# Offsets, features and sampled keys by chunks of channels, in small steps inside the main loop, with the depthwise taps on VectorE

## The chip, the cores and the metric

The kernel runs on one core of one Trainium2 chip. The metric is the device time of one execution in microseconds; each figure is a median of several executions. All executions used here are in the fast state. "TensorE" is PE in the profile, "VectorE" is DVE, "ScalarE" is ACT, "GpSimd" is POOL. SBUF and PSUM are the on-chip memories that hold the kernel's tiles: its matmuls write PSUM tiles, and an "evacuation" is the ScalarE instruction that takes a finished PSUM tile to SBUF, with its ReLU (1.11 to 1.20 us each in the kernel before). The "granted clock" of a view is the share of TensorE's full clock that the profile shows.

## The reference, cut to what matters

The input has 2 images, 512 channels, 32 by 32 pixels. A depthwise 6x6 convolution with stride 4 over the queries gives offsets. At the offset positions the normalised input is sampled (64 keys per group). A bias network of two hidden layers of 128 runs on every pair of a pixel and a key, and that is nearly all the work.

```python
xn  = bn(x); q = grouped_1x1(xn, qw)
off = gelu(depthwise_6x6_stride4(q) + b)        # the 36 taps
off = tanh(off_pw @ off) * 4
kv  = grid_sample(xn, grid + off); k, v = ...   # the sampling
pos = grid_q - grid_kv
bias = sign(pos) * log1p(abs(pos))              # the features
bias = relu(bias @ w1 + b1); bias = relu(bias @ w2 + b2); bias = bias @ w3 + b3
attn = softmax(q k^T * scale + bias); x = x + out(attn v); x = x + mlp(bn(x))
# then one full attention layer over the 1024 pixels
```

## The kernel before

Everything up to the features is done for all channels at once, ahead of the main loop. The depthwise convolution is 36 matmuls with diagonal weights:

```python
for b in range(B):
    for k in range(NCH):          # 8 chunks of 128 channels: normalise, q, transposes
        ...
pc = pp.tile([P, 512], F32, tag="ps", name="pc")
for t in range(KS * KS):          # 36 taps on TensorE (72 in the profile)
    dg = ph2.tile([P, P], F32, name="dg", bufs=4)
    nc.vector.tensor_scalar(dg, ident, col("dww", t), None, ALU.mult)
    ky, kx = divmod(t, KS)
    nc.tensor.matmul(pc.rearrange(...), dg, qpad[:, :, ky : ky + 29 : 4, kx : kx + 29 : 4],
                     start=(t == 0), stop=(t == KS * KS - 1))
... # gelu, offsets, weights, sampling, keys, values, features; all chunks
```

The main loop has 256 steps. This is its order in both kernels:

```python
for s in range(NS):
    if s > 0: st_sum(s - 1, 2)                    # VectorE, 2nd sum of the step before
    if s % 4 == 0: st_tables(s // 4 + 1)          # DMA + two ScalarE ops: ta, tb (2 buffers)
    st_layer1(s + 2)                              # VectorE: h1 of 4096 elements (3 buffers)
    st_layer2(s)                                  # TensorE: 32 matmuls; ScalarE evacuates 4 PSUM tiles
    st_sum(s, 0)                                  # VectorE, 1st sum
    ...                                           # every 2nd step: layer 3; per group: softmax
```

The evacuations write `rx` (3 buffers), `ua` (5) and `ub` (4); three PSUM tiles of 128x1024 f32 serve layer 2 and, in the changed kernel, the background work too. Each matmul of the program appears as two MATMUL instructions in these profiles (16384 for layer 2, which is 256 steps of 32). The order in which an engine runs its instructions needn't be the order of the text: in the kernel before, VectorE ran a sign test of line 163 at 4.95 us and the first normalisation of line 118 at 7.48. Where it is said below that the build puts an instruction first or early, such an order is meant; by what rule it comes about, no run here shows.

## Time and profile before

| | before |
|---|---|
| time, median of 3 executions | 2977.14 us |
| head, up to the first layer-2 matmul | 180.66 us |
| loop, first layer-2 matmul to the end of the last | 1908.2 us |
| rest (projections, MLP, second layer) | 887.9 us |

The three parts below the first line are read from the profiled execution, which spans 2976.7 us. The profile's group lines give busy time in us and the mean of one instruction in ns, then the engine's idle time just before these instructions and what ended most of it. The lines themselves are shown in the prediction. The reading in one sentence: TensorE has no idle time in the loop (1908.20 us busy of 1908.20), and VectorE has half a microsecond to spare in a step (0.48 us, as the prediction works it out).

### The profile page before, as it was taken

What the parts mean: (1) busy time and instruction counts of PE and PEld (TensorE: products, weight loads), DVE (VectorE), ACT (ScalarE), POOL (GpSimd) and SP (SyncE); (2) the same over time, 40 slices, a digit from 0 to 9 for tenths busy, and PEclk for the clock granted to TensorE, in tenths of its full rate; (3) what the DMA queues carried; (4) which work ended last, traced back from release to release, by engine and by line L of the source; (5) the groups of instructions that cost most, each with busy time, mean ns of one, the idle gap of its engine ahead of it and who ended that gap; (6) DMA issues with size and microseconds to landing.
All of it is one profiled execution on the core that took longest, in us unless ns stands there. A gap on an engine that the chain in (4) does not pass through costs nothing.

```text
span 2976.7 us, 45771 instructions
## 1 busy us (share of the span) xinstructions
PE 2916.3 (98%) x20316; PEld 1059.9 (36%) x20316; DVE 1971.8 (66%) x1200; ACT 1439.9 (48%) x1381; POOL 221.3 (7%) x264
## 2 busy tenths in 40 slices
PE   8679999999999999999999999999999999999999
PEld 3323333333333333333333333335444444454444
DVE  3389999999999999999999999998200100013031
ACT  1346766666666766666667676666201011010010
POOL 0001111111111111111111111111000000000000
PEclk9889999999999999999999999999999999999999
DMA  2024444444444444444444444444200100000000
GB/s 89 0 61 93 86 96 83 93 86 93 86 93 86 93 86 93 86 93 86 93 86 93 85 92 88 89 106 111 113 0 0 57 0 0 0 0 1 28 1 29
DMA packets 59893, 197.48 MB, mean 66 GB/s; under 512 B 10288, under 2 KB 10544, under 8 KB 58544
## 3 DMA queue, kind: packets, MB, share of 16 engines
q0 software_dynamic: 36576, 133.19, 23.6%
q1 hardware_dynamic: 22544, 60.04, 6.9%
q8 instruction: 160, 2.62, 0.4%
q10 hardware_dynamic: 576, 1.34, 0.1%
q14 instruction: 37, 0.30, 0.0%
HBM read 56.91 MB, written 4.46 MB: 21 GB/s over the span
## 4 chain that ended last, share of the span: by engine, by line
PE 97%; DVE 1%; ACT 1%; DMA 0%; SPq 0%; issue 0%; ACTq 0%; DVEq 0%
PE ps L358 59%; PE psm L514 7%; PE psh L506 7%; PE sim L394 4%; PE pss L586 4%; PE psa L636 4%; PE pc L149 2%; PE psp L575 2%; PE pso L486 2%; PE psv L625 2%; PE psg L551 1%; PE pkv L242 1%; PE psq L123 1%; PE sim L384 1%; PE psx L605 0%; PE psu L560 0%
## 5 line engine op out<-in xcount | busy, mean ns | idle before, releaser
L358 PE MATMUL ps<-h,cw 128*32 128x512 f32 x16384 | 1792.9, 593 | 17.8 <-DVE h L341 17.8
L341 DVE CUSTOM_DVE_ANT_1 h<-ta,tb 128x4096 f32<-128x4096 f32 x256 | 1132.6, 4425 | 119.0 <-PE ps L358 102.3
L358 PEld LDWEIGHTS ps<-h,cw 128*32 128x32 f32 x16384 | 554.0, 110 | 1225.4 <-issue 1186.4
L364 ACT ACTIVATE rx<-ps,sc 128x1024 f32<-128x1024 f32 x512 | 570.2, 1114 | 326.5 <-PE ps L358 325.8
L366 ACT ACTIVATE ua<-ps,sc 128x1024 f32<-128x1024 f32 x256 | 308.3, 1204 | 152.5 <-PE ps L358 152.5
L366 ACT ACTIVATE ub<-ps,sc 128x1024 f32<-128x1024 f32 x256 | 307.9, 1203 | 115.3 <-PE ps L358 115.3
L374 POOL DMA_DIRECT2D ua<-ub x254 | 218.6, 861 | 1856.2 <-DVE ub L372 1840.2
L372 DVE SCALAR_TENSOR_TENSOR ua<-rx,sc,ua 128x1024 f32<-128x1024 f32 x256 | 327.6, 1280 | 14.4 <-ACT ua L366 14.1
L372 DVE SCALAR_TENSOR_TENSOR ub<-rx,sc,ub 128x1024 f32<-128x1024 f32 x256 | 327.3, 1279 | 5.6 <-ACT ub L366 5.6
L518 DVE SCALAR_TENSOR_TENSOR xs<-psm,vs,xs 128x512 f32<-128x512 f32 x16 | 12.0, 752 | 425.7 <-PE psm L514 425.7
L506 PE MATMUL psh<-xn,w_s 128*128 128x512 f32 x512 | 220.4, 592 | 0.0
L514 PE MATMUL psm<-hm,w_s 128*128 128x512 f32 x512 | 220.4, 592 | 0.0
L510 ACT ACTIVATE hm<-psh,vs 128x512 f32<-128x512 f32 x64 | 44.0, 687 | 364.0 <-PE psh L506 364.0
L506 PEld LDWEIGHTS psh<-xn,w_s 128*128 128x128 f32 x512 | 97.3, 190 | 122.4 <-issue 122.4
L514 PEld LDWEIGHTS psm<-hm,w_s 128*128 128x128 f32 x512 | 97.3, 190 | 122.4 <-issue 122.4
L394 PE MATMUL sim<-ua,w3s 128*32 128x512 f32 x1024 | 136.7, 593 | 0.0
L586 PE MATMUL pss<-xs,qs 128*128 128x512 f32 x256 | 112.2, 592 | 0.0
L636 PE MATMUL psa<-aT,vt 128*128 128x512 f32 x256 | 110.2, 592 | 0.0
L327 ACT ACTIVATE ta<-fb,vs 128x512 f32<-128x512 f32 x64 | 89.7, 1401 | 20.9 <-DMA fb<-fdr 16.1
L592 DVE TENSOR_REDUCE mx<-pss 128x1 f32<-128x1024 f32 x16 | 19.6, 1225 | 117.8 <-PE pss L586 117.8
L579 ACT ACTIVATE qs<-psp,ub 128x512 f32<-128x512 f32 x16 | 11.0, 687 | 137.8 <-PE psp L575 137.8
L641 DVE SCALAR_TENSOR_TENSOR res<-psa,ub,xs 128x512 f32<-128x512 f32 x16 | 12.0, 751 | 97.3 <-PE psa L636 97.3
(134 smaller groups left out, 1051.0 us busy)
## 6 DMA issues: line engine op xcount, KB each, us to landing
ua<-ub POOLq DMA_DIRECT2D x254, 512.0 KB, 4.7
fb<-fdr SPq DMA_DIRECT2D x64, 512.0 KB, 5.3
w_s<-in_w SPq DMA_DIRECT2D x8, 1024.0 KB, 12.1
x<-in_x SPq DMA_DIRECT2D x8, 512.0 KB, 8.0
xs<-in_x SPq DMA_DIRECT2D x16, 256.0 KB, 6.8
wl_s<-in_wl SPq DMA_DIRECT2D x4, 1024.0 KB, 7.9
out<-res SPq DMA_DIRECT2D x16, 256.0 KB, 2.0
vp<-in_outw SPq DMA_DIRECT2D x1, 1024.0 KB, 9.3
```

The costliest lines, as they stand in the source:

```text
L327: nc.scalar.activation(ta.rearrange("p j x -> p x j"), fb[:, 0], AF.Identity, bias=col("cb1"), scale=col("w1x"))
L341: nc.vector._custom_dve(TENSOR_ADD_SAT, out=h1.rearrange("p y t x -> p (y t x)"), in0=ta[:, j : j + 4, :].rearrange("p t x -> p (t x)").un ...
L358: nc.tensor.matmul(ps[32 * q : 32 * q + 32, h, :], cw2[:, 32 * z : 32 * z + 32], h1[:, 16 * h : 16 * h + 16, q, :], start=True, stop=True,)
L364: nc.scalar.activation(o, ps, AF.Relu, bias=sc[:, 4 + z : 5 + z])
L366: nc.scalar.activation(o, ps, AF.Relu, bias=sc[:, 4 + z : 5 + z], scale=sc[:, z : z + 1])
L372: nc.vector.scalar_tensor_tensor(r[1], r[0], sc[:, z : z + 1], r[1], ALU.mult, ALU.add)
L374: nc.gpsimd.dma_start(out=sums[s][1], in_=sums[s][3], accum_op=ALU.add)
L394: nc.tensor.matmul(sims[gi][q : q + 32, :], w3s[:, 28 - 4 * i : 60 - 4 * i], sums[s + e][z][:, h, :], start=False, stop=(i == NSL // 2 - 1 ...
L506: nc.tensor.matmul(ps, w1_s[:, k, i * P : (i + 1) * P], xn2[:, k, :], start=(k == 0), stop=(k == NCH - 1),)
L514: nc.tensor.matmul(ps, w2_s[:, i, o * P : (o + 1) * P], hm[:, i, :], start=(i == 0), stop=(i == NF - 1),)
L586: nc.tensor.matmul(ps[:, h, :], qs[:, k, t * P : (t + 1) * P], xs[:, k, b, h * 512 : (h + 1) * 512], start=(k == 0), stop=(k == NCH - 1),)
L636: nc.tensor.matmul(ps, vt[:, m, o * P : (o + 1) * P], aT[:, m, n], start=(m == 0), stop=(m == 7),)
```

## The change

The intent is to start the loop as soon as the first 128 channels have their features, and to do the other seven chunks' work beside the loop, in the slack of the other engines. The channels are split into five chains (one, one, two, two, two chunks). A generator does a little of the work in each step of the loop. The taps become multiply-add operations of VectorE on the SBUF copy of q.

```diff
+CHAINS = [[(0, 0)], [(0, 1)], [(0, 2), (0, 3)], [(1, 0), (1, 1)], [(1, 2), (1, 3)]]
+TAPS = 3
-        for t in range(KS * KS):
-            nc.vector.tensor_scalar(dg, ident, col("dww", t), None, ALU.mult)
-            nc.tensor.matmul(pc.rearrange(...), dg, qpad[...], ...)
+        def chain(ci):                      # load, normalise, q, taps, gelu, offsets, features
+            ...
+            for m, t in enumerate(taps):
+                for src, dst in ops:        # qa in steps of 4 pixels; two ops at the y edges
+                    if m == 0:
+                        nc.vector.tensor_scalar(dst, src, col("dww", t), None, ALU.mult)
+                    else:
+                        nc.vector.scalar_tensor_tensor(dst, src, col("dww", t), dst, ALU.mult, ALU.add)
+                if ci > 0 and m % (2 * TAPS // K) == 2 * TAPS // K - 1:
+                    yield                   # 6 taps a step for one chunk, 3 for two
+            ...
+        def sample(ci): ...                 # weights, transposes, sampling, keys, values
+        def later():
+            yield from sample(0)
+            for ci in range(1, len(CHAINS)):
+                yield from chain(ci)
+                yield from sample(ci)
+        for _ in chain(0): pass             # only the first chunk ahead of the loop
 ...
+        bg = later()
         for s in range(NS):
             ...
             st_sum(s, 0)
+            next(bg, None)
```

Small preparations (weight signs, scales) move from VectorE to GpSimd, and the products of q and k close a group's accumulation instead of opening it.

## The prediction

> **What bounds the kernel now.** I read the page first, then five windows, then single stretches of the order in time.
>
> The engine rows and the costliest groups of the page:
> ```profile
> PE 2916.3 (98%) x20316; PEld 1059.9 (36%) x20316; DVE 1971.8 (66%) x1200; ACT 1439.9 (48%) x1381; POOL 221.3 (7%) x264
> L358 PE MATMUL ps<-h,cw 128*32 128x512 f32 x16384 | 1792.9, 593 | 17.8 <-DVE h L341 17.8
> L341 DVE CUSTOM_DVE_ANT_1 h<-ta,tb 128x4096 f32<-128x4096 f32 x256 | 1132.6, 4425 | 119.0 <-PE ps L358 102.3
> ```
> TensorE is busy throughout; its largest group waited 17.8 us in all, VectorE waited 102.3 us for TensorE. I then cut the span at the taps, the end of the taps, the first layer-2 matmul and the last layer-3 matmul (start:end, length, then busy us and instructions of each engine, granted clock, DMA share, GB/s):
> ```profile
> 0.00:34.30 34.30, 23.67 (x96) 14.29 (x96) 22.40 (x96) 10.80 (x18) 2.71 (x10) 1.00 0.49 192
> 34.30:100.40 66.10, 66.10 (x75) 15.31 (x74) 10.20 (x34) 1.24 (x2) 0.00 (x0) 1.00 0.00 0
> 100.40:180.60 80.20, 35.87 (x308) 25.24 (x306) 43.39 (x41) 34.87 (x43) 0.00 (x0) 0.74 0.07 17
> 180.60:2092.50 1911.90, 1911.19 (x17652) 603.07 (x17652) 1781.53 (x843) 1309.06 (x1195) 218.61 (x254) 1.00 0.45 90
> 2092.50:2976.70 884.20, 879.47 (x2191) 402.01 (x2188) 114.29 (x189) 83.97 (x126) 0.00 (x0) 0.99 0.05 19
> ```
> So there are 180.6 us of head: 34 of loading and q, 66 of the depthwise taps as 72 TensorE matmuls, 80 of offsets, sampling and features with TensorE less than half busy. Then the loop: 256 steps in 1911.9 us, 7.47 us each, with no TensorE idle. Last comes the rest, also TensorE. Whatever TensorE work moves into the loop is therefore paid in full; whatever moves to the other engines costs only what exceeds their slack.
>
> That slack, in VectorE's order over two steps:
> ```profile
> 430.52 4.43 DVE L341 CUSTOM_DVE_ANT_1 h<-ta,tb 128x4096 f32<-128x4096 f32 x1
> 434.86 1.28 DVE L372 SCALAR_TENSOR_TENSOR ub<-rx,sc,ub 128x1024 f32<-128x1024 f32 x1
> 436.06 1.28 DVE L372 SCALAR_TENSOR_TENSOR ua<-rx,sc,ua 128x1024 f32<-128x1024 f32 x1
> 438.24 4.43 DVE L341 CUSTOM_DVE_ANT_1 h<-ta,tb 128x4096 f32<-128x4096 f32 x1 [0.91 <-PE ps L358]
> ```
> VectorE works 6.9 us of a step and waits 0.91 us in every second one, for TensorE to free an h1 buffer. Between 280 and 2000 us its groups' idle sums to 110 us over 231 steps: 0.48 us a step, softmax included. ScalarE's busy time in the loop, 1309 of 1912 us, leaves 2.3 us a step.
>
> The end of the head, which stays in the changed kernel:
> ```profile
> 164.83 2.85 SPq L300 DMA_DIRECT2D fdr<-late  x4
> ...
> 174.41 1.25 ACT L327 ACTIVATE ta<-fb,vs 128x512 f32<-128x512 f32 x1 [12.64 <-DMA fb<-fdr]
> ...
> 180.66 1.08 PE L358 MATMUL ps<-h,cw 128*32 128x512 f32 x4 [17.78 <-DVE h L341]
> ```
> From the write of the features to the first layer-2 matmul: 15.8 us of write, broadcast read, tables and first h1.
>
> [...] the three-operand operation takes 0.751 us for 512 elements (L641) and 1.280 for 1024 (L372), 1.033 ns an element and 0.222 us fixed. [...] each load here takes 1283 ns. Each chain adds a Gelu and an Ln set and softmax comes back to Exp. [...] the first four q matmuls took 3.75 us, later fours 1.88.
>
> **The change part by part.**
>
> *New head.* Only chunk (0,0) goes through it.
> - x, 512 KB: similar transfers in the loop land in 4.7 to 5.3 us; with 0.7 of issue and company, ready at 6.0 us. Normalisation on ScalarE 1.1: 7.2. Four cold q matmuls 3.8: 11.0. One copy of 1024 elements 1.1: 12.1.
> - 36 taps, each needing the one before. A dependent pair starts 0.03 after the first ends (L214 starts at 105.96 for 1.23, L218 on its result at 107.22). So 0.222 + 64 x 1.033 ns + 0.03 = 0.32; 36 of them, 11.4 us: 23.5.
> - Gelu 0.3, six small projections on a cool TensorE 1.2, two tanh 0.7, offsets 1.3: 27.0. Features on 128 columns instead of 1024: pos, Abs, u 0.8; then Ln with its load (1.6) beside the reciprocal chain (reciprocal 6.54 us per 1024, so about 1.0 here; 1.9 in all); two closing operations 0.7: 30.4.
> - The 15.8 us above, 0.7 less for a smaller write: first layer-2 matmul at **45.5 us**, instead of 180.66.
>
> GpSimd now takes 67 sign/swap operations and the BN scale. [...]
>
> *The fixed rest.* From 180.66 to 2976.7: **2796.0 us**, the same work.
>
> *TensorE work moved into the loop,* per chunk: q four matmuls at 0.44 (L273: 7.03/16) 1.76; eight transposes 1.04; pkv 32 x 0.068 (16.51/242) 2.18; kv keys 2 x 0.12 = 0.25; values 0.88: 6.1 us, 48.9 for eight. Less what runs before the loop starts, when TensorE is free (q and sampling of chunk 0, q of chunk 1): 7.9. Plus four sets of projections 2.4, and the first group's q.k products, which used to precede 180.66, 0.9. Sum **44 us**. The 66 us of tap matmuls vanish and are inside the head already.
>
> *VectorE in the loop.* Taps: chain 1 11.4. A two-chunk chain has 24 merged taps of 128 elements at 0.385 and 12 edge taps of two operations, about 0.5 a pair: 15.2 us, three times. Weights 7 x 1.23 = 8.6; offsets and features about 6.6 for each large chain and 4 for the small one. Sum about 11 + 46 + 9 + 24 = 90 us, spread by the count of yields over steps 0 to 105. Slack there: 106 x 0.48 = 51, plus the 44 that TensorE gains: 95. It just fits in total, but not at every moment: twelve tap steps bring 15.2/12 = 1.27 us against 0.48, a lag of 9.5 us; the feature steps bring about 3 more. The buffers absorb a part: h1 is made at least a step early (h1 of step s+2 starts when step s does, needs 4.4 of 14.9 us), but rx has three buffers, so a sum delayed by some 7 us stops ScalarE, then PSUM. So about 4 us lost in each of three large chains, 2 in the small one: 14. ScalarE pieces of 1.1 us and eight or more table loads ahead of evacuations, 3 more. **17 us**.
>
> *End.* The new xs lies over h1 and tables, not over qpad, so x is loaded at the loop's end instead of earlier. Such a load takes 6.8 us; the first product needs it about 5 us after the loop, and there are three PSUM buffers: **1 us**.
>
> Sum: 45.5 + 2796.0 + 44 + 17 + 1 = 2903.5. The profiled span and the median differ by 0.4; I say 2903.
>
> **The rivals.**
> 1. *TensorE remains without bubbles.* For it: softmax already puts 2.9 us on VectorE within a few steps and costs under 1 us, and the trace shows that instructions don't run in the order of the text (the sign tests of line 163 ran before the normalisation of line 118), so taps may fill the 0.91 us waits early, and chain 1 may do its taps while the first tables travel. Then 2886 us.
> 2. *VectorE bounds every tap and feature step,* because nothing can be made ahead. Excess over slack: 11.4 - 2.9 = 8.5 for chain 1's taps, 3 x 9.5 for the others, features and offsets 14, weights 5: 56 us instead of 14. Then 2945, still within 2% of before. Against it: the wait of 0.91 us shows VectorE is ahead of TensorE.
> 3. *GpSimd is late.* At 1 us an operation its 67 end at 76 us, and layer 2 needs cw2 and the scales: head 76, total about 2934. Memsets of 60 elements take 0.15 us, which speaks against 1 us.
> 4. *TensorE waits in its queue for ScalarE or VectorE* at each of some 35 new products. Half a microsecond each is 17 us on top: 2920. The yields between producer and consumer speak against it.
>
> **Range and chances.** 2% below is 2917.6 us. The gain is 180.66 - 45.5 = 135 of head, less 62 given back. The head is uncertain by some 6 us, the moved work by 4, the stalls from 0 to 50, upwards. Range 2884 to 2934. Faster by over 2%: 0.74; within 2%: 0.24; slower: 0.02.
>
> **What would show it.** First layer-2 matmul at 42 to 50 us, its last releaser h1 and not a GpSimd result; no tap matmuls; VectorE's busy share in the first 800 us of the loop at 95% or more, later back to 93; TensorE idle in the loop of 10 to 25 us, mostly behind VectorE or evacuations during taps and features of the chains with two chunks; steps after about 106 at 7.47 us again; last layer-3 to end 884 us. I am wrong if the first layer-2 matmul comes after 60 us, if steps in the second half are longer than before, or if TensorE idles over 40 us in the loop.

## The result, and the profile after

The changed kernel takes **2938.29 us** (2935.70 to 2938.86, 4 runs); the kernel before took 2978.53 in the same rounds. The ratio is 0.9865 (95% interval 0.9847 to 0.9882), 1.3% faster: less than predicted and outside the range. A ratio here is the mean time of one kernel's fast runs over that of the other's of the same rounds, so not quite the ratio of the medians.

The engine rows and the two largest groups of the changed kernel:

```profile
PE 2868.2 (98%) x20300; PEld 1023.2 (35%) x20300; DVE 1993.7 (68%) x1321; ACT 1482.4 (51%) x1505; POOL 233.7 (8%) x337
L377 PE MATMUL ps<-h,cw 128*32 128x512 f32 x16384 | 1806.1, 595 | 32.2 <-DVE h L360 15.0
L360 DVE CUSTOM_DVE_ANT_1 h<-ta,tb 128x4096 f32<-128x4096 f32 x256 | 1131.2, 4419 | 85.0 <-PE ps L377 76.9
```

The layer-2 group (L358 before, L377 now) waits 32.2 us instead of 17.8. VectorE waits 76.9 us for TensorE instead of 102.3: its slack has shrunk, but the total looks far from used up. The span cut at the first layer-2 matmul, at the end of the moved work (step 106) and at the last layer-2 matmul (start:end, length, then busy us and instructions of PE, PEld, DVE, ACT, POOL, granted clock, DMA share, GB/s):

```profile
0.00:48.25 48.25, 11.24 (x25) 4.89 (x26) 21.29 (x52) 16.16 (x28) 13.61 (x76) 0.69 0.24 83
48.25:927.80 879.55, 856.58 (x7728) 276.08 (x7732) 821.83 (x588) 617.79 (x656) 91.92 (x112) 0.99 0.40 85
927.80:2046.30 1118.50, 1117.36 (x10340) 339.49 (x10336) 1034.99 (x493) 763.29 (x695) 128.18 (x149) 1.00 0.43 87
2046.30:2933.90 887.60, 883.05 (x2220) 402.76 (x2212) 115.56 (x190) 85.19 (x127) 0.00 (x0) 0.99 0.06 24
```

| | before | after | |
|---|---|---|---|
| head | 180.66 | 48.25 | -132.4 |
| loop | 1908.2 | 1998.0 | +89.8 |
| of it the first 106 steps | 790.5 | 879.5 | +89.0 |
| rest | 887.9 | 887.7 | -0.2 |

So the head gave nearly what was expected, steps after 106 and the rest are unchanged, and nearly the whole difference from the prediction lies in the 106 steps that carry the moved work. TensorE idles there 879.55 - 856.58 = 23.0 us; before, it idled none. The half-speed time of the granted clock in the loop grew from 3.0 to 21.2 us.

The end of the head, in order of time, to set against the same lines of before:

```profile
35.25 2.66 SPq L249 DMA_DIRECT2D fdr<-fe  x4
...
41.90 1.25 ACT L346 ACTIVATE ta<-fb,vs 128x512 f32<-128x512 f32 x1 [4.03 <-DMA fb<-fdr]
...
48.25 1.08 PE L377 MATMUL ps<-h,cw 128*32 128x512 f32 x4 [15.00 <-DVE h L360]
```

The features leave at 35.25, 4.9 us later than predicted, and the way from there takes 13.0 us instead of 15.1; the last thing waited for is h1, as it should be.

One of the stops of TensorE in a tap step, in order of time (instructions left out):

```profile
528.09 1.29 ACT L346 ACTIVATE ta<-fb,vs 128x512 f32<-128x512 f32 x1 [4.95 <-DVE h L360]
...
529.78 1.10 ACT L383 ACTIVATE rx<-ps,sc 128x1024 f32<-128x1024 f32 x1
...
530.92 11.40 PE L377 MATMUL ps<-h,cw 128*32 128x512 f32 x92 [2.94 <-ACT rx L383]
```

ScalarE stands at the table build `ta`, which overwrites a buffer that VectorE's h1 still reads. It waits 4.95 us. The evacuation of a finished PSUM tile stands behind it in the queue: the tile that the `rx` at 529.78 reads was finished at 523.59, and ScalarE ran nothing from 523.14 to 528.09. The other two PSUM tiles were finished at 525.30 and 527.99, and TensorE, out of PSUM tiles, stops for 2.94 us. There are ten such stops in the 106 steps, of 0.7 to 3.7 us each and 22.7 in all: five behind `ta` (12.7 us in all), one behind the Gelu (3.65), one behind the exponential (1.72), one behind the load of chain 1 (2.51), two others. And a stop costs more than itself (windows around this one; the third figure from the right is the granted clock):

```profile
528.00:530.90 2.90, 0.00 (x0) 0.00 (x0) 2.86 (x5) 2.81 (x4) 0.86 (x1) 0.89 0.02 8
530.90:532.00 1.10, 1.07 (x8) 0.40 (x12) 1.10 (x2) 1.10 (x2) 0.00 (x0) 0.50 0.92 212
534.00:535.00 1.00, 1.00 (x16) 0.36 (x12) 1.00 (x1) 0.75 (x1) 0.00 (x0) 1.00 1.17 233
```

After the stop the clock is granted at half (0.50) and 8 matmuls start in 1.1 us where later 16 start in 1.0. The lapse lasts 3.41 us, so it costs 1.7 us; it follows five of the stops. Which stops it follows can be read from the traces: all changes of the clock lie on a grid of 3.413 us, and in the loops of all 19 traces 56 of 58 lapses follow a grid stretch in which TensorE was idle for 2.04 us or more, while no stretch that idle went without one (the other two follow 1.66 and 1.91 us, at the Gelu's stop). In the changed kernel the five lapses follow stretches with 2.15 to 2.64 us idle; the stops of 2.30 and 2.51 us fall across two stretches, with at most 1.64 and 2.02 us in one, and have no lapse; the one of 2.15 us falls into one stretch and has one.

### The profile page after: what moved, and what is told of

It reads as the page before. It is cut to its first block, busy times and chain, and to the rows that moved or that the text cites. A ratio compares the mean times of both kernels' runs of the same rounds, so it can differ in the third digit from the quotient of the medians.

```text
span 2933.9 us, 46008 instructions
## 1 busy us (share of the span) xinstructions
PE 2868.2 (98%) x20300; PEld 1023.2 (35%) x20300; DVE 1993.7 (68%) x1321; ACT 1482.4 (51%) x1505; POOL 233.7 (8%) x337
## 4 chain that ended last, share of the span: by engine, by line
PE 88%; DVE 8%; issue 3%; ACT 1%; DMA 1%; SPq 0%; ACTq 0%; DVEq 0%
PE ps L377 52%; PE psm L535 7%; PE psh L527 7%; PE pss L607 4%; PE psa L657 4%; DVE h L360 4%; PE sim L414 3%; PE psp L596 2%; PE pso L507 2%; PE psv L646 2%; DVE acc L202 1%; DVE ub L391 1%; DVE ua L391 1%; PE psg L572 1%; PE pkv L291 0%
## 5 line engine op out<-in xcount | busy, mean ns | idle before, releaser
L377 PE MATMUL ps<-h,cw 128*32 128x512 f32 x16384 | 1806.1, 595 | 32.2 <-DVE h L360 15.0
L360 DVE CUSTOM_DVE_ANT_1 h<-ta,tb 128x4096 f32<-128x4096 f32 x256 | 1131.2, 4419 | 85.0 <-PE ps L377 76.9
L377 PEld LDWEIGHTS ps<-h,cw 128*32 128x32 f32 x16384 | 537.0, 110 | 1259.5 <-issue 1196.7
L346 ACT ACTIVATE ta<-fb,vs 128x512 f32<-128x512 f32 x64 | 87.9, 1374 | 45.0 <-DVE h L360 36.5
```

Of the source, the lines that this page charges most:

```text
L346: nc.scalar.activation(ta.rearrange("p j x -> p x j"), fb[:, 0], AF.Identity, bias=col("cb1"), scale=col("w1x"))
L360: nc.vector._custom_dve(TENSOR_ADD_SAT, out=h1.rearrange("p y t x -> p (y t x)"), in0=ta[:, j : j + 4, :].rearrange("p t x -> p (t x)").un ...
L377: nc.tensor.matmul(ps[32 * q : 32 * q + 32, h, :], cw2[:, 32 * z : 32 * z + 32], h1[:, 16 * h : 16 * h + 16, q, :], start=True, stop=True,)
```

## The experiments

Diffs are abridged here: patterns and names are shortened. Three theories were held in turn, and the expectations on record name them by letter. They call the changed kernel "the tap version", and sometimes say "chunk" for chain. **A**: VectorE's sums come late, so that `rx` buffers run out. **B**: table loads and other ScalarE pieces delay evacuations. **C**: an instruction of ScalarE that waits for late VectorE work holds back the evacuations that stand behind it in ScalarE's order. The trace of the changed kernel shows this at each of the five stops behind `ta`: the next evacuation started 5.3 to 6.7 us after its PSUM tile was finished, right behind the tables (6.19 us at the stop shown). **D** came later: VectorE has no time left in tap steps. In each run below, stops and half-clock time are those of TensorE in the loop; in the changed kernel they are 24.0 and 21.2 us, and the loop is 1998.0 us.

### e1_few_taps: only the first tap of chains 1 to 4

```diff
             for m, t in enumerate(taps):
+                if ci > 0 and m > 0: (yield as before) continue
```

The result is wrong on purpose, though it passed the tolerance.

> Wrong result on purpose: in chains 1 to 4 only the first of the 36 taps is done, everything else stays where it is. Theory A (VectorE's taps come faster than its slack, its sums fall behind, ScalarE runs out of rx buffers, TensorE stops[...]): the seven waits in tap steps, 18 us, and the five clock lapses, 8.5 us, go; from 2938 to 2910 to 2917 us. Theory B (ScalarE's table loads and added pieces hold up the evacuations): unchanged, 2934 to 2940.

Measured: 2908.81 us, ratio 0.9764 (0.9750 to 0.9779). Stops 6.1 us, half clock 4.4, loop 1969.7. So the taps on VectorE cost 29 us, in line with theory A (1 us below its range) and not with B. In the changed kernel these taps keep VectorE busy for 60.0 us, so about half of that was absorbed. Without them the loop is 1969.7 - 1908.2 = 61.5 us longer than before, which is what the prediction had for everything.

### e2_no_tables: Gelu and Ln of chains 1 to 4 replaced by functions of tables already loaded

```diff
-AF.Gelu / AF.Ln
+AF.Gelu if ci == 0 else AF.Tanh / AF.Ln if ci == 0 else AF.Abs
```

The result is wrong on purpose here too.

> Wrong result on purpose: in chains 1 to 4 Gelu becomes Tanh and Ln becomes Abs, so that ScalarE changes its table less often; all durations but the loads stay. Theory A: within 4 us of 2938. Theory B: 10 us or more less, below 2928.

Measured: 2935.91 us, ratio 0.9854 (0.9840 to 0.9869); loop 1995.7. The edit did what it was to do: 13 table loads of 1.28 us in the first 106 steps became one. The time is within the scatter of the changed kernel: theory B falls.

### e3_rx4: a fourth buffer for rx

```diff
-bufs=(3, 5, 3, 4)[z]
+bufs=(4, 5, 4, 4)[z]
```

> Right result: four rx buffers in place of three. Theory A: a sum may be late by another 3.4 us (half a step) before ScalarE stops, so about half of the stops go: 2920 to 2930. Theory B: no change, since evacuations held up by ScalarE itself are not helped by rx: 2934 to 2940.

Measured: 2936.73 us, ratio 0.9856 (0.9839 to 0.9872); loop 2000.9, stops 27.5. Theory A in this form falls.

### e4_spread: 4, 2, 1 and 1 taps a step instead of 6, 3, 3, 3

```diff
-                if ci > 0 and m % (2 * TAPS // K) == 2 * TAPS // K - 1:
+                if ci > 0 and m % PER_STEP[ci] == PER_STEP[ci] - 1:      # [0, 4, 2, 1, 1]
```

> Right result: the same taps in more steps: 4 a step in chain 1 (was 6), 2 in chain 2 and 1 in chains 3 and 4 (was 3). Theory A: 1 tap of two chunks is about 0.5 us a step, near the slack of 0.48, so chains 3 and 4 stop no more, chains 1 and 2 less: 2914 to 2924. Theory B: the same loads and pieces come, only later: 2934 to 2940.

Measured: 2943.31 us, ratio 0.9877 (0.9863 to 0.9892); loop 2004.7, stops 29.8. At first this looked like proof that the density of taps does not matter. It was not: the run did not do what its text says, as the held spread below shows.

### e5_early: the first chunk's sampling and chain 1's beginning ahead of the loop

```diff
+        for _ in range(8):
+            next(bg)
         for s in range(NS):
```

> Right result: the sampling of chunk 0, the q of chunk 1 and its first six taps stand before the loop in the text. If they failed to run early only because their PSUM buffers come after those of step 0 in the text, 6 us of TensorE work leave the loop, and the stop behind the normalisation of chunk 1 (2.5 us) goes: 2928 to 2932, the head longer by less than 2 us. Otherwise unchanged.

Measured: 2935.42 us, ratio 0.9853 (0.9838 to 0.9868). The head is 49.07 us. TensorE's sampling work did move out of the loop, but a new stop of 10.98 us, ending at 106 us, came where VectorE did 17 taps in a row while layer 3 waited for a sum, and another of 1.76. What was gained was lost there; the expected 2928 to 2932 did not come.

### e6_contig: taps read neighbouring pixels (wrong on purpose)

```diff
-xs_                                   # every fourth pixel, 16 bytes apart
+slice(4 + kx, 4 + kx + x1 - x0)       # contiguous, for chains 1 to 4
```

> Wrong result on purpose: in chains 1 to 4 the taps read eight neighbouring columns in place of every fourth. If the stride of 16 bytes is what makes them long, 128 elements take 0.35 to 0.38 us in place of 0.449 and 64 take 0.29 in place of 0.327; VectorE is 8 us less busy, and under theories A and C some of the stops go: 2922 to 2934. If not, all stays.

Measured: 2927.64 us, ratio 0.9825 (0.9810 to 0.9840). The same instruction, in the changed kernel and then here (groups by shape):

```profile
L202 DVE SCALAR_TENSOR_TENSOR acc<-qa,vs,acc 128x128 f32<-128x128 f32 x45 | 20.2, 449 | 1.0
```

```profile
L202 DVE SCALAR_TENSOR_TENSOR acc<-qa,vs,acc 128x128 f32<-128x128 f32 x45 | 15.7, 349 | 1.0
```

The stride of 16 bytes costs 0.10 us per tap of 128 elements, 449 against 349 ns. VectorE's busy time in the first 106 steps fell by 11.1 us (856.4 to 845.3, durations summed), the median time by 10.7 and the profiled execution by 8.2: most of what is taken from VectorE in these steps comes back in the time. It isn't one for one in general, since e1 took away some 58 us and gained 29. This was the first hint of theory D.

### e10_ta3: a third buffer for ta and tb

```diff
-name="ta", bufs=2 / name="tb", bufs=2
+name="ta", bufs=3 / name="tb", bufs=3
```

> Right result: three buffers of the tables ta and tb in place of two. Theory C (the first four runs led to it: [...] whenever VectorE is late, an instruction of ScalarE that needs VectorE holds back the evacuations behind it, and TensorE stops; five of the seven long stops come 3 us after a ta that waited 4 to 5 us for an h1 to free its buffer): those five stops, 12.7 us, and four clock lapses, 6.8 us, go: 2916 to 2925. Theory A (the sums late for rx): unchanged, 2934 to 2941.

Measured: 2938.56 us, ratio 0.9862 (0.9846 to 0.9878). The build now asks for each table one chunk earlier, and waits at the same place for the same h1: at 298 us it was 4.2 us before and 4.10 here. More buffers do not make VectorE faster: h1 takes 4419 ns in both.

### e11_tables_pool: the tables on GpSimd

```diff
-            nc.scalar.activation(ta.rearrange(...), fb[:, 0], AF.Identity, bias=..., scale=...)
+            nc.gpsimd.tensor_scalar(ta.rearrange(...), fb[:, 0], col("w1x"), col("cb1"), ALU.mult, ALU.add)
```

(the same for `tb`; the first chunk stays on ScalarE)

> Right result: the tables ta and tb of all chunks but the first are made on GpSimd, so that no evacuation stands behind their wait. Theory C: the five ta stops go as with a third buffer, and ScalarE gains 2 us per four steps: 2914 to 2926, if GpSimd doesn't slow VectorE. Theory A: unchanged or slower, 2934 to 2945.

Measured: 3044.62 us, ratio 1.0220 (1.0202 to 1.0238), slower than before. Two groups of this kernel:

```profile
L355 POOL TENSOR_SCALAR ta<-fb,vs 128x512 f32<-128x512 f32 x63 | 243.0, 3857 | 441.2 <-issue 374.8 <-DVE h L369 38.5 <-DMA fb<-fdr 27.9
...
L423 PE MATMUL sim<-ua,w3s 128*32 128x512 f32 x1024 | 202.8, 615 | 64.4 <-DMA ua<-ub 64.3
```

A table takes GpSimd 3.86 us (ScalarE: 1.37). GpSimd also starts the accumulating transfers of `ub` into `ua`; they come late, and layer 3 waits 64.3 us for them. Both ranges were missed, and the run says nothing for or against C, because it brings its own wait.

### e14_tables_behind and e15_all_behind: ScalarE's order changed

The first issues the two table builds behind the step's last evacuation. The second does so with every ScalarE instruction of the background work and softmax, with one step more before the exponential and one before the normalisation.

```diff
+            with tc.issue_after(ev[s]):      # order of issue only, no wait
+                st_tables(s // 4 + 1)
 # e15 only:
+            with tc.issue_after(ev[s]):
+                next(bg, None); next(tail, 0)
```

> The tap version with one difference: the two table builds of a chunk are held in ScalarE's order behind the last evacuation of the step in which the text asks for them, so that they cannot be queued ahead of evacuations while VectorE still reads the buffer that they overwrite. Theory C (ScalarE's in-order queue: an instruction that waits for late VectorE work stands ahead of the evacuations that TensorE needs): the five stops of TensorE behind the first table build (2.3 to 2.9 us each, 13.3 us in all) go, and with them about four lapses of the clock at 1.7 us, so 2918 to 2926, gaps of TensorE in the loop about 10 us. Rival theory D (VectorE's taps simply leave too little VectorE time there, and the wait shows up wherever the queue happens to be): the stops move to other ScalarE instructions or to the evacuations themselves and the time stays at 2935 to 2940.

> As the run with the tables behind the evacuations, and also every ScalarE instruction of the background work and of the softmax is held behind the last evacuation of its step, with one more step between the subtraction and the exponential and one more between the load of a chunk of channels and its normalisation. Theory C: nearly all stops in the loop (22.9 us) and the half clock after them (some 8 us) go: 2905 to 2914, close to the kernel with one tap a chunk (2908.8), gaps in the loop under 7 us, half clock under 8 us. Theory D: the stops stay, at the evacuations instead (waits of ScalarE for VectorE before a first-row evacuation), and the time is 2930 to 2940.

Measured: 2934.94 us, ratio 0.9849 (0.9833 to 0.9866) for the tables; 2976.36 us, ratio 0.9989 (0.9981 to 0.9998) for all. The table group of e14, and then a stop in the same kernel:

```profile
L349 ACT ACTIVATE ta<-fb,vs 128x512 f32<-128x512 f32 x64 | 88.1, 1377 | 3.9 <-DMA fb<-fdr 3.9
```

```profile
569.03 0.40 ACT L206 ACTIVATE gof<-acc,vs 128x128 f32<-128x128 f32 x1 [4.25 <-DVE acc L202]
...
570.49 3.97 PE L380 MATMUL ps<-h,cw 128*32 128x512 f32 x20 [3.11 <-ACT rx L386]
```

The tables no longer wait for VectorE at all (36.5 us before). All five stops behind them are gone, as theory C asks. And the loop is 1998.2 us, the same as without the edit. The waiting has moved to the Gelu (28.6 us of waits for the taps, 17.4 before) and to the evacuations. Theory C named where the stops stand, not why there are stops. e15 missed both ranges, by 36 us and more. Of its 45.9 us of stops, 27.4 are layer 3 waiting for the accumulating transfers, 7.8 products of the background work that came late, and 6.1 the transposes behind softmax; why the transfers were late was not looked into.

### What was left: theory D

One view that I should have cut earlier: the changed kernel between 489.0 and 578.4 us, the eleven tap steps of chain 3.

```profile
489.00:578.40 89.40, 84.31 (x755) 24.77 (x758) 88.90 (x82) 57.46 (x54) 9.48 (x11) 0.96 0.37 78
```

VectorE (third busy figure) works 88.90 of 89.40 us. In every run of tap steps, 7 to 13, 25 to 34, 53 to 63 and 81 to 97, its waits of over 0.15 us sum to 0.00 (each run ends with steps for the offsets and features behind the last tap). In e1, without the taps, VectorE waits 4.5, 6.9, 5.3 and 6.7 us in these four runs of steps, and TensorE doesn't stop in them. Its order there, against the two steps of before:

```profile
507.24 4.42 DVE L360 CUSTOM_DVE_ANT_1 h<-ta,tb 128x4096 f32<-128x4096 f32 x1
511.58 1.28 DVE L391 SCALAR_TENSOR_TENSOR ub<-rx,sc,ub 128x1024 f32<-128x1024 f32 x1
512.77 1.28 DVE L391 SCALAR_TENSOR_TENSOR ua<-rx,sc,ua 128x1024 f32<-128x1024 f32 x1
513.97 0.90 DVE L202 SCALAR_TENSOR_TENSOR acc<-qa,vs,acc 128x112 f32<-128x112 f32 x2
514.78 4.42 DVE L360 CUSTOM_DVE_ANT_1 h<-ta,tb 128x4096 f32<-128x4096 f32 x1
```

From start to start, h1 and two sums take 513.97 - 507.24 = 6.73 us, so the 7.30 us that TensorE needs on average in a quiet step leave 0.57. Chain 3's taps take 16.2 us of VectorE in these eleven steps (overlaps counted once), 1.5 a step. So VectorE falls behind by 0.9 us a step; the buffers bridge some of it (VectorE's second sum starts 3.8 us after the end of its evacuation in step 52, before the taps, and 8.3 in step 56, the last before the stop), and then somebody must wait. Who it is depends on ScalarE's queue (the tables in the changed kernel, the Gelu and the evacuations in e14); how much changed little with more buffers or with the tables moved (loops of 1998.2 to 2000.9 us in e3, e10 and e14), but the orders of e15 and e20 cost more. In the sampling steps between (44 to 50, say), VectorE waits 0.7 to 2.9 us a step, which is why the average of 93.4% (821.83 of 879.55) shows nothing.

### e16_spread_held: 3, 2, 1, 1 taps a step, each held behind the first sum of its step

```diff
-                if ci > 0 and m % (2 * TAPS // K) == 2 * TAPS // K - 1:
+                if ci > 0 and m % PER_STEP[ci] == PER_STEP[ci] - 1:      # [0, 3, 2, 1, 1]
+                with tc.issue_after(last_first_sum):   # order of issue on VectorE, no wait
                     for src, dst in ops: ...
```

> 3, 2, 1 and 1 taps a step in the chunks 1 to 4, and each tap held on VectorE behind the first sum of its step, so that the build cannot put the taps in bursts as in the first spread run (no taps in steps 72 to 97 there, 12 in one step before). Theory D (VectorE has no time left in tap steps): with one tap a step (0.45 to 0.9 us beside 6.96 us of sums and h1 in steps of 7.3 us) the debt of chunks 3 and 4 stays under the 9 us that the buffers bridge, so the four stops of TensorE there (9.6 us) and their clock lapses (6.8 us) go, chunks 1 and 2 keep one or two: 2915 to 2925. Theory C: in-order waits remain wherever gof, the exponential and the tables stand: 2933 to 2943 as in the first spread run.

Measured: **2915.80 us**, ratio 0.9792 (0.9775 to 0.9808), as theory D expects. Stops 12.2 us, half clock 6.5, loop 1978.7. The taps of chain 3 by themselves, in two windows each (us of VectorE and count come first after the length); first in e4_spread, then in this run:

```profile
564.30:648.10 83.80, 16.19 (x48) 0.40 (x1) 0.98 0.35 72
648.10:840.20 192.10, 0.00 (x0) 0.00 (x0) 1.00 0.44 89
```

```profile
573.10:693.80 120.70, 7.49 (x22) 0.00 (x0) 1.00 0.40 84
693.80:844.00 150.20, 9.25 (x26) 0.00 (x0) 1.00 0.44 90
```

In e4 the text asked for one tap a step, but all 48 operations ran in ten steps and none in the next 26: the build had put them first. So e4 was no spread at all. Here they are spread, and the steps of chain 4 are back at the TensorE pace (ten steps of this run with one tap each, 7.30 us a step):

```profile
1114.10:1187.10 73.00, 73.00 (x684) 22.10 (x680) 71.22 (x40) 49.35 (x44) 8.60 (x10) 1.00 0.42 85
```

### e20_held: the hold alone, at 6 and 3 taps a step

```diff
                 if ci > 0 and m % (2 * TAPS // K) == 2 * TAPS // K - 1:     # as in the change
+                with tc.issue_after(last_first_sum):
                     for src, dst in ops: ...
```

> The tap version's own 6 or 3 taps a step, each held on VectorE behind the first sum of its step; nothing spread. Theory D (the debt per run of tap steps decides): the debt is the same as in the tap version, so the stops stay in number if not in place, 2930 to 2940. Rival theory E (the burst of taps that the build puts first, 12 in one step, is what makes h1 and the sums late, and the hold alone cures it): 2912 to 2922, as the held spread.

Measured: 2952.45 us, ratio 0.9909 (0.9896 to 0.9923); stops 36.3 us, half clock 34.7, loop 2014.7. The hold alone is worse than nothing: chain 1's taps now trail, and one stop (at 174 us, layer 3 behind an accumulating transfer) lasts 10.2 us. So it is the spread that helps (some 35 us between this run and e16), and the hold is only what makes the spread real. Rival E falls. The run came out still slower than theory D's 2930 to 2940, so the debt isn't all; the order in which it is served counts too.

### e17_pool_taps: the held spread, taps on GpSimd

```diff
+                            nc.gpsimd.tensor_scalar(tv, src, col("dww", t), None, ALU.mult)
+                            nc.gpsimd.tensor_tensor(dst, dst, tv, ALU.add)
```

> The same spread, but the taps of chunks 1 to 4 on GpSimd, each as a product and a sum, held behind the accumulating transfer of the step before. Theory D: VectorE loses all the added work, the stops of tap steps go, and the time comes near the run with one tap a chunk (2908.8), if GpSimd keeps up: a 512-element operation took it 3.9 us, so about 1 us for 128 elements, 2 us a tap, up to 6 us a step. Rival: the operations delay GpSimd's accumulating transfers by that much, and the sums that layer 3 and the evacuations wait for come late, as with the tables on GpSimd: 2935 to 2980.

Measured: 2980.65 us, ratio 1.0012 (1.0003 to 1.0021). The rival of that run is right in its mechanism, and the time just above its range. One of its groups:

```profile
L206 POOL TENSOR_SCALAR tmp<-qa,vs 128x128 f32<-128x128 f32 x45 | 128.4, 2868 | 0.0
```

A product of 128 elements takes 2.87 us and the sum 1.93, 4.8 us a tap instead of 0.45; the accumulating transfers stand behind them (layer 3 waits 28.5 us for them, of 53.2 us of stops). A GpSimd operation of the same size in the head takes 0.54 us, contiguous and with VectorE less busy; which of the two makes the difference, no run here separates.

### e18_phase and e19_phase_held: q stored grouped by x modulo 4

A legal version of e6: the copy from PSUM writes q so that each tap reads runs of 8 elements; the product of q and k reads it back in order. e19 has the held spread too.

```diff
-                nc.scalar.copy(qa[:, b, k, :], ps)
+                nc.scalar.copy(qa[:, b, k, :] as (y c x), ps as (y x c))
-                            qa[:, b, k, h * 512 : (h + 1) * 512], start=False, stop=False,
+                            qa[...].rearrange("p (y c x) -> p y x c", y=16, c=4), start=False, stop=False,
```

> The tap version with q stored grouped by x modulo 4 (the copy from PSUM writes it so, the products of q and k read it back in order), so that every tap reads runs of 8 elements, with right results. Theory D: as the wrong-on-purpose contiguous run, 10 us less: 2926 to 2930, tap of 128 elements 0.35 us. Against it: the copy of q or the 128 matmuls that now read with a stride take longer; over 0.2 us per matmul would eat the gain (26 us).

> Held spread and grouped layout together. Theory D: the debt of chunk 2 also comes near what the buffers bridge; 2905 to 2918, all stops in tap steps of chunks 3 and 4 gone. Theory C: 2922 to 2932, the layout's gain alone.

Measured: 2938.85 us, ratio 0.9867 (0.9852 to 0.9882), and 2924.21 us, ratio 0.9815 (0.9800 to 0.9830): no gain over the changed kernel, and 8 us lost to the held spread. The taps are as short as hoped (350 ns), and the copy takes 1013 ns as before. The products of q and k, in the changed kernel and in e18:

```profile
L405 PE MATMUL sim<-qa,kz 128*32 128x512 f32 x128 | 16.7, 594 | 0.0
```

```profile
L409 PE MATMUL sim<-qa,kz 128*32 128x512 f32 x128 | 32.6, 1098 | 0.0
```

A moving operand read in strides of 32 bytes takes TensorE 1098 ns instead of 594, 15.9 us busy in all. That is more than the taps gave: stops fell from 24.0 to 16.1 us and half clock from 21.2 to 15.3 us. The trace of the kernel before could have warned: its tap matmuls, which read q in steps of 16 bytes, take 1092 ns each. e19 falls into theory C's range, but not for C's reason: the products cost it the same 15.9 us, and its stops are down to 6.3 us, with none over 0.6 us in the tap steps of chains 3 and 4.

### e23_own_xn and e21_best: two further steps from the held spread

```diff
-tag="xn", name="xn")
+tag="xn" if ci else "xn0", name="xn")     # e23: chunk 0's channels in a buffer of their own
+        for _ in range(5): next(bg)        # e21 also: the first chunk's sampling ahead of the loop
```

> The held spread with a buffer of its own for the first chunk's channels, so that chunk 1's load need not wait for the first chunk's transposes. If the stop of 3.0 us at 75 us and its 4.6 us of ScalarE waiting for the transfer come from that buffer, they go, with their clock lapse: 3 to 6 us less than the held spread, 2910 to 2914. Rival: the transfer is late for the queue that issues it, not for the buffer, and nothing changes: 2914 to 2918.

> The run with the buffer of its own, and the first chunk's sampling before the loop, where TensorE waits for h1 anyway (none of chunk 1's taps with it, unlike the earlier run with an early start). That run lost 12.7 us to two stops and still gained 1 to 3 us, so 5 to 12 us less than the run before this: 2900 to 2909. Rival: the sampling's VectorE work (a product of 1024 elements) delays the first h1, and the head grows by what the loop loses: 2909 to 2915.

Measured: **2912.61 us**, ratio 0.9776 (0.9763 to 0.9790) for e23; 2916.49 us, ratio 0.9790 (0.9777 to 0.9803) for e21. In the held spread, ScalarE and then TensorE waited for chain 1's channels:

```profile
72.81 1.24 ACT L172 ACTIVATE xn<-xn,vs,bns 128x1024 f32<-128x1024 f32 x1 [4.62 <-DMA xn<-in_x]
...
75.20 5.22 PE L379 MATMUL ps<-h,cw 128*32 128x512 f32 x32 [3.04 <-ACT ua L387]
```

With the buffer of its own, TensorE runs through (the stop and its clock lapse are gone), as expected; the ratios' intervals of the held spread and of e23 overlap, so the gain of some 3 us rests on the traces. Sampling ahead of the loop then brings nothing, and e21 lies outside both of its ranges: the head grew by only 0.15 us, but stops in the loop grow from 8.5 to 15.2 us. That everything behind it comes at other times and meets other work is argued, not shown. e23 beats both kernels, by 2.2% and, against the changed kernel's median, by 25.7 us.

## Why the prediction was wrong

The mechanism was the predicted one, VectorE falling behind in the tap steps; the step that failed is what the buffers absorb, and with it the term for stalls. The sum, term by term (moved work is the time from one matmul's start to the next, without stops and half clock; stalls are what remains of the loop's 89.8 us):

| term | predicted | measured |
|---|---|---|
| head | 45.5 | 48.25 |
| fixed rest | 2796.0 | 2796.1 |
| TensorE work moved | 44 | 50.1 |
| stalls | 17 | 39.7 |
| end | 1 | -0.2 |
| sum | 2903.5 | 2933.9 |

- **The head** was right to 2.8 us, with two errors that offset each other: features 4.9 us late, the way from them to layer 2 some 2 us shorter.
- **Moved TensorE work.** Its sizes were right. What failed is "less what runs before the loop starts": the first chunk's sampling and chain 1's q ran in the loop, which is the 6.1 us, because they stand behind the loop's first steps in the text: in e5, which puts them before, the moved work in the loop is 44.1 us instead of 50.1. That their PSUM tiles are the reason is argued.
- **The taps' cost.** A large chain's taps took 16.2 us instead of 15.2. A tap of 128 elements took 0.449 us where the fit (0.222 + 128 x 0.001033) gives 0.354: the fit came from contiguous operands, and the taps read a stride of 16 bytes. The operations at the edges came cheaper, since two of them for different chunks overlap (at 495 us, operations of 56 elements that take 0.30 to 0.31 us start 0.22 us apart), so that the taps of chains 1 to 4 took 60.0 us where 57 were predicted. e6 puts the stride by itself at 8 to 11 us of the time. It is part of the stalls.
- **Stalls, the step that failed.** "The buffers absorb a part" and "about 4 us lost in each of three large chains, 2 in the small one" were too hopeful. The debt was predicted rightly, 9.5 us for a large chain against 11 x 0.9 measured; the buffers bridged less of it than assumed, and what stopped was not `rx` (a fourth buffer in e3 changed nothing) but whatever stood ahead of the evacuations in ScalarE's queue. Stops and the clock lapses after them came to 5.4 us in chain 1 and 7.2, 9.9 and 6.2 in chains 2 to 4, and 2.5 for the load of chain 1. I had left the lapses out: of 21.2 us at half clock 1.0 fell into stops, so they cost (21.2 - 1.0) / 2 - 3.0 / 2 = 8.6 us more than before. With 24.0 of stops in the whole loop that is 32.6 of the 39.7. The other 7 lie between layer-2 matmuls, in pieces too short to count as stops: from start to start they take 1774.7 us, against 1767.4 before and 1772.4 in e1. So 5 of the 7 are there without the taps too; their cause stays open.
- **Rivals.** Rival 2, VectorE bounds every tap step, at 2945, described the mechanism (e1, e6, e16), and is 7 us too high. Rival 3's 2934 is nearer to the measured 2938.29, by luck, since what it describes did not happen. I had set rival 2 aside because VectorE waits 0.91 us for TensorE before; that wait says how much slack there is, not that 1.5 us of new work a step fit in it. Rival 1 fell, and so did the mechanism of rival 3: GpSimd ended its preparation at 22.97 us, with 67 operations of 0.22 us each on average from 9.90 us on. Rival 4 holds only for the Gelu of chain 1, where a projection itself waited 3.65 us.
- **Signs.** First layer-2 matmul between 42 and 50: yes. TensorE idle of 10 to 25 us in the loop: yes, and yet the time was wrong, since idle is only part of what a stop costs. Busy share of VectorE at 95%: 93.4, an average over two kinds of step, saturated in one and waiting in the other. Steps after 106 and the tail: as said.

Shown by runs: that the taps on VectorE cause the loss (e1), that loads, `rx`, table buffers and table order don't (e2, e3, e10, e14), and that truly spreading them recovers most of it (e16 against e20 and e4). Argued only: how many us of debt the buffers can bridge (the 9 us in the expectation of e16 is my estimate), and what the last 7 us come from.

## What to carry to other kernels

Slack is to be counted in each kind of step, against the work that this step gets; an average over steps with and without the work hides a saturated engine (VectorE: 88.90 of 89.40 us in chain 3's tap steps, 93.4% on average), and removing the wait where it shows only moved it here (e14). Spreading work thinly over more steps was worth more than buffers here (22.5 us against none), but the order in the text does not make it so: look in the trace at when the instructions really ran, and hold them in the queue if the build bunches them. A stop of TensorE of 2 to 3 us should be priced with the slow clock that can follow it, 1.7 us here.
